# Deformable layer of a fused network: eight taps over 4x4 cells in place of four taps over 4x8, and x hats in two halves

## The chip, the cores and the metric

The kernel runs on one core of one Trainium2 chip. The metric is the device time of one execution in microseconds, the median of several runs. Engine names: PE is TensorE (PEld its weight load), DVE is VectorE, ACT is ScalarE, POOL is GpSimd, SP is SyncE, which here only issues DMAs. Everything is fp32.

## The reference, cut to what matters

The network has four residual layers on x of shape 8 x 384 x 32 x 32 (samples, channels, height, width): a state-space layer, a deformable convolution, a state-space layer with an MLP, and a displacement layer. Only the second is touched. Its core, cut:

```python
def sample(py, px):            # bilinear; corners outside the image count 0
    y0, x0 = floor(py), floor(px)
    dy, dx = py - y0, px - x0
    return (corner(y0, x0, (1 - dy) * (1 - dx)) + corner(y0, x0 + 1, (1 - dy) * dx)
            + corner(y0 + 1, x0, dy * (1 - dx)) + corner(y0 + 1, x0 + 1, dy * dx))
def deform_block(x, ow, ob, dw, pw, pb, K):
    offsets = conv2d(x, ow, ob, K // 2)          # 2*K*K channels: dy, dx of each tap
    acc = 0
    for k in range(K * K):                       # the taps; same offsets for all 128 channels
        acc += sample(gy + ky[k] + offsets[2 * k], gx + kx[k] + offsets[2 * k + 1]) * dw[k]
    return conv2d(acc, pw, pb, 0)                # 1x1
# layer: groupnorm, channels split in three groups of 128 with K = 3, 5, 7, outputs
# concatenated, times a squeeze-and-excite weight, plus x
```

## The kernel before, in words

**The sampling as a matrix product.** A bilinear corner weight is a product of two hats, max(0, 1 - |py - yc|) and max(0, 1 - |px - xc|), for the pixel (yc, xc) read. So for each tap the sampled image of 128 channels is a matrix product: rows of the image's pixels (the contraction, on the partitions) with a matrix "pixel by output position" of hat products. Offsets are bounded (RAD is 2, 3, 4 for K = 3, 5, 7), so a small cell of pixels can only reach a small window of output positions. A cell before is 4 rows by 8 columns, 32 pixels; four taps are stacked on the 128 partitions (a *quad*, `QUADS`). The image has 8 x 4 such cells. K*K = 9, 25, 49 taps give 2, 6, 12 quads, and one tap left over, which is done alone with whole rows as cells (4 rows x 32 pixels, 8 cells).

**The pipeline of one quad.** SP fetches the positions of its four taps from DRAM, each row copied to the 32 partitions of its tap (`positions`, tile `fpyx`, two buffers; the DRAM rows are written by `offsets` or `fir_end` and called `fposd`). ACT makes hats of x (`fhx`, L1573 Abs and L1579 Relu) and of y (`fhy`, L1586 Abs and L1591 Relu); one Abs per cell column or row, one Relu for the tile, two buffers each. DVE multiplies the pixels of the cells, 8 x 128 channels at a time, by the tap's weights (`weigh`, L1609, out `fxk`, four buffers, from the cells `fxt` and the broadcast weights `fwk`) and hat by hat (`product`, L1626, out `fsm`, five buffers, one instruction for cells of equal height). PE multiplies (`products`, L1657), each cell into its window of `wacc`: five PSUM banks of 16 rows that overlap by 8 rows[...].

**A block** is one sample b and one group g (K = 3, 5, 7). At its end ACT copies outer rows of `wacc` out (`sums_act`, L1381), DVE adds the others (`sums`, L1386), both into `fdsb`, and only then may PE start the next block, as `wacc` has one buffer. Then PE does the 1x1 convolution, and ACT and DVE the squeeze.

**Units and slots.** A quad is done in two units, the upper and the lower four rows of cells; a unit is `(b, g, j, h)`. There are 6, 14 and 26 units for K = 3, 5, 7: 46 a sample, 368 in all. The list of units is the clock of the layer. In slot u PE does unit u, DVE weighs and multiplies unit u+1, ACT makes the hats of unit u+2 (x and y hats of a quad together with its upper half), and SP fetches positions four units ahead. The order on PE, DVE and ACT is as written (`tc.manual_schedule`); POOL's and SP's follows from the scheduler. All else is put into slots by `put(slot, place, ...)`: places `act0`, `pe0`, `dve0` stand ahead of the unit's work on that engine, `act1`, `dve1`, `pe1` behind it. With s0 the first slot of a block:

```python
put(s0 - 5, "dve1", cells_map)      # image reordered to cells, fxp<-fxn, 8 copies on POOL (L1335)
put(s0 - 4, "pe1", rows_pe)         # transposes, pixels to partitions
put(s0 - 3, "act0", cells_out)      # to DRAM (fxd)
for q in range(4):                  # and back, copied for the four taps: 4 tiles fxt4 of 0.5 MB
    put(s0 - 1 + q // 2, "dve0", cells_in, q)
put(end, "act0", sums_act)
put(end, "dve0", sums)
```

The offset convolutions are put beside the units of the blocks ahead: K = 7 in slots 0 to 13 of its own sample (`fir`, L1267), K = 5 in slots 34 to 39 and K = 3 at once in slot 5 (`conv`, L1305), both for the next sample. Slots are counted here from the first 3x3 unit of a sample; the 5x5 block starts at slot 6, the 7x7 block at slot 20.

The functions that the change touches, and what calls them:

Of the kernel before, what the change touches and what calls it, by code (L numbers as in the profile page):

```python
# [15 lines left out]
P = 128  # L16
# [36 lines left out]
NX = 4  # L53
# [8 lines left out]
HXN, HYN, SMN = 2080, 1792, 896  # L62
# [3 lines left out]
def box(y, x, h=2, w=2):  # L66
# [3 lines left out]
QUADS = {  # L70
    3: [box(-1, -1), [(-1, 1), (0, 1), (1, 0), (1, 1)], [(1, -1)]],
    5: [box(y, x) for y in (-2, 0) for x in (-2, 0)] + [box(2, -2, 1, 4), box(-2, 2, 4, 1), [(2, 2)]],
    7: [box(-3, -3), box(-3, -1), box(-1, -3, 1, 4), box(-3, 2), box(-1, 2), box(-3, 1, 4, 1)]
    + [box(0, -3), box(2, -3), box(0, -1, 4, 1), box(2, 0), box(2, 2), box(1, 0, 1, 4), [(0, 0)]],
# [14 lines left out]
def taps_of(K):  # L89
    return [(y + K // 2) * K + x + K // 2 for q in QUADS[K] for y, x in q]  # L90

# [5 lines left out]
class Net:  # L97
# [956 lines left out]
    def deform_fast(self, src, dst):  # L1054
        tc, nc, ins = self.tc, self.nc, self.ins
        with ExitStack() as ctx:
# [9 lines left out]
            for g, K in enumerate(KS):  # L1066
                K2, (n, st, cols) = K * K, CONV[K]
                rows = 2 * K2
                queue = nc.scalar if K == 7 else nc.sync
                ow = wp.tile([P, K * NFIR if n == 1 else K2, rows if n == 1 else st], F32, name=f"fow{K}")  # L1070
                ob = wp.tile([P, 1], F32, name=f"fob{K}")
                obk = wp.tile([P, 1], F32, name=f"fobk{K}")
                grid = wp.tile([P, cols], F32, name=f"fgrid{K}")
                for t in (ob, obk, grid) + ((ow,) if n > 1 else ()):
                    nc.gpsimd.memset(t, 0.0)
                if n == 1:
                    self.fir_weights(ow, ins[f"ow{K}"])
                else:
                    queue.dma_start(out=ow[:, :, :rows], in_=ins[f"ow{K}"])
                for i in range(n):  # L1080
                    r = slice(i * st, i * st + rows)
                    queue.dma_start(out=ob[r], in_=ins[f"ob{K}"])
                    queue.dma_start(out=obk[r], in_=ins["c_cols"][:rows, Q_K + g : Q_K + g + 1])
                    queue.dma_start(out=grid[r], in_=ins["c_grid"][:rows, i * cols : (i + 1) * cols])
                if n == 1:
                    nc.gpsimd.tensor_scalar(grid[:rows], grid[:rows], obk[:rows], None, ALU.add)
                nc.vector.tensor_tensor(obk, obk, ob, ALU.add)
                nq = K2 // 4
                wk = wp.tile([P, nq + 1, P], F32, name=f"fwk{K}")
                for t in range(4):  # L1090
                    queue.dma_start(
                        out=wk[H * t : H * (t + 1), :nq, :],
                        in_=ins[f"dw{K}"][t : 4 * nq : 4, :].partition_broadcast(H),
                    )
                queue.dma_start(out=wk[:, nq, :], in_=ins[f"dw{K}"][4 * nq, :].partition_broadcast(P))
                self.f[K] = (ow, ob, obk, grid, wk)
# [8 lines left out]
            self.cell = wp.tile([P, 13], F32, name="cell")  # L1105
# [13 lines left out]
            for b in range(self.nb):  # L1119
                for g in range(G):  # L1120
                    first[b, g] = len(units)
                    units += [(b, g, j, h) for j in self.order(g) for h in range(2)]
# [12 lines left out]
            with tc.manual_schedule(engines=engines):  # L1135
                for u in range(min(slots), max(slots) + 1):
# [4 lines left out]
                    now, after, hats, grid = (unit(u + k) for k in (0, 1, 2, 4))  # L1141
                    if grid and grid[3] == 0:
                        self.positions(*grid)
# [5 lines left out]
                    if dve:  # L1149
                        dve.pop(0)()  # L1150
# [4 lines left out]
                    if hats:  # L1155
                        self.unit_hats(*hats)
# [30 lines left out]
    def block_steps(self, b, g, first, put, weights, src, dst):  # L1187
# [10 lines left out]
        end = first[b, g + 1] if g < G - 1 else first[b, 0] + sum(2 * len(QUADS[k]) for k in KS)  # L1198
# [51 lines left out]
        def fir_sum():  # L1250
            xs = s["xs"] = self.q1.tile([P, H, W // 2], F32, name="fxs")
# [20 lines left out]
        def fir_take(part):  # L1272
            ps = s["ps"][:used]
            if part == 0:
                s["fs"] = self.q1.tile([P, HL], F32, name="ffs")
                nc.scalar.activation(s["fs"][:used], ps, AF.Identity, bias=ob[:used])
                return
# [52 lines left out]
        def cells_map():  # L1330
            xp = s["xp"] = self.q1.tile([P, L], F32, name="fxp")
            x5 = xg().rearrange("p (by yl bx xl) -> p by yl bx xl", yl=4, bx=NX, xl=W // NX)
            p5 = xp.rearrange("p (by yl xl bx) -> p by yl bx xl", yl=4, bx=NX, xl=W // NX)
            for by in range(NT):
                nc.gpsimd.tensor_copy(p5[:, by], x5[:, by])  # L1335
# [17 lines left out]
        def cells_in(q):  # L1353
            xt = s[q] = self.q1.tile([P, NX, 2, P], F32, name="fxt4", tag="fxt4", bufs=4)
            src = s["xd"].rearrange("(c x) y o -> c x y o", x=NX)[:, :, 2 * q : 2 * q + 2]
            n = P // NX
            for t in range(4):
                nc.sync.dma_start(out=xt[n * t : n * (t + 1)], in_=src)
# [91 lines left out]
        if g == 0:  # L1450
            t = s0 - 2 * len(QUADS[KS[-1]])
# [34 lines left out]
        for q in range(4):  # L1486
            put(s0 - 1 + q // 2, "dve0", cells_in, q)
# [29 lines left out]
    def order(self, g):  # L1517
        n = len(QUADS[KS[g]])
        return [n - 1] + list(range(n - 1))

# [8 lines left out]
    def ends(self, g):  # L1529
        last = {}  # L1530
        for j in self.order(g):
            _, _, yw, xw = self.windows(g, j)
            for half in range(2):
                for bx in range(len(xw)):
                    for by in range(4 * half, 4 * half + 4):
# [4 lines left out]
    def windows(self, g, j):  # L1540
        K = KS[g]
        taps, R = QUADS[K][j], RAD[K]
        one = len(taps) == 1
        bw, nbx = (W, 1) if one else (8, NX)
# [6 lines left out]
    def positions(self, b, g, j, half):  # L1551
        s = self.state[b, g]
        taps = QUADS[KS[g]][j]
        pyx = s["pyx", j] = self.q2.tile([P, 2, L], F32, name="fpyx", tag="fpyx")
        n = P // len(taps)
        for t, _ in enumerate(taps):
            self.nc.sync.dma_start(
                out=pyx[n * t : n * (t + 1)],
                in_=s["posd"][8 * j + 2 * t : 8 * j + 2 * t + 2, :].partition_broadcast(n),
            )  # L1560

    def unit_hats(self, b, g, j, half):
        nc, s = self.nc, self.state[b, g]
        taps, one, yw, xw = self.windows(g, j)
        pyx = s["pyx", j]
        if half == 0:
            hx = self.q2.tile([P, HXN], F32, name="fhx", tag="fhx")
            at, hx_at = 0, []
            px = pyx[:, 1, :].rearrange("p (h w) -> p h w", w=W)
            for bx, (xa, xb) in enumerate(xw):  # L1570
                w = xb - xa
                bias = self.cell[:, 12:13] if one else self.cell[:, 8 + bx : 9 + bx]
                nc.scalar.activation(  # L1573
                    hx[:, at : at + H * w].rearrange("p (h w) -> p h w", w=w), px[:, :, xa:xb],
                    AF.Abs, bias=bias,
                )
                hx_at.append(at)
                at += H * w
            nc.scalar.activation(hx[:, :at], hx[:, :at], AF.Relu, bias=self.col(Q_ONE), scale=-1.0)  # L1579
            s["hx", j] = hx, hx_at  # L1580
        hy = self.q2.tile([P, HYN], F32, name="fhy", tag="fhy")
        at, hy_at = 0, {}
        for by in range(4 * half, 4 * half + 4):
# [3 lines left out]
                hy[:, at : at + (yb - ya) * W], pyx[:, 0, ya * W : yb * W], AF.Abs, bias=bias  # L1587
# [4 lines left out]
        s["hy", j, half] = hy, hy_at  # L1592


    def unit_dve(self, b, g, j, half):
# [3 lines left out]
        hx, hx_at = s["hx", j]  # L1599
        hy, hy_at = s["hy", j, half]  # L1600
        xk = s["xk", j, half] = []
        sets = s["sets", j, half] = []

        def weigh():
            for q in (2 * half,) if one else (2 * half, 2 * half + 1):
                t = self.q2.tile([P, 2 * NX, P], F32, name="fxk", tag="fxk", bufs=4)
                n = 4 if one else 2 * NX
                x = s["xt1"][:, 4 * half : 4 * half + 4, :] if one else s[q].rearrange("p x y o -> p (x y) o")
                nc.vector.tensor_tensor(t[:, :n], x, wk[:, j : j + 1, :].to_broadcast([P, n, P]), ALU.mult)  # L1609
                xk.append(t)  # L1610

        def product(bx, part):
# [4 lines left out]
            for by in part:  # L1617
# [17 lines left out]
            sets.append((bx, part, sm, sm_at))  # L1635

        bys = range(4 * half, 4 * half + 4)
        parts = [bys[:2], bys[2:]] if one else [bys]
        return [weigh] + [
            lambda bx=bx, part=part: product(bx, part) for bx in range(len(xw)) for part in parts  # L1640
        ]

    def unit_pe(self, b, g, j, half):
        nc, s = self.nc, self.state[b, g]
        taps, one, yw, xw = self.windows(g, j)
        xk = s["xk", j, half]
        ends = self.ends(g)

        def products(bx, part, sm, sm_at):
            xa, xb = xw[bx]  # L1650
            w = xb - xa
            for by in part:
                ya, yb = yw[by]
                o = self.bank(ya)
                k = xk[0][:, by % 4] if one else xk[(by - 4 * half) // 2][:, 2 * bx + by % 2]
# [8 lines left out]
        return [lambda a=a: products(*a) for a in s["sets", j, half]]  # L1664
# [255 lines left out]
def lay_out(inputs):  # L1920
# [49 lines left out]
    cell = [4 * np.arange(NT)[None, :] + p[:, None] % 32 // 8, 8 * np.arange(NX)[None, :] + p[:, None] % 8]  # L1970
    cell.append(p[:, None] % NX * (W // NX) + p[:, None] % W // NX)
# [26 lines left out]
```

## Time and profile before

| what | value |
|---|---|
| median of 3 runs | 9035.51 us (9035.41 to 9037.79) |
| the profiled execution: time, span | 9039.51 us, 9037.7 us |
| mean granted TensorE clock in it | 0.914 |
| deformable layer in the span | first matmul of L1657 at 2881.6 us, last at about 5469 us |
| columns of all L1657 matmuls, all L1626 products | 852,912 each |
| L1657 PE, busy | 1663.5 us, twice 5312 records |
| L1626 DVE, L1609 DVE, busy | 1170.1 us, 785.7 us |
| L1573 and L1586 ACT (Abs), busy | 407.6 us, 645.1 us |

The profile is of one execution, so a sum over its rows is compared with its own time, 9039.51 us. An fp32 matmul leaves two records in the trace. "Busy" counts the union of an engine's instructions, the mean ns of one its own length, which for pipelined matmuls is more than the distance from one to the next. Idle time before a group is put down to the instruction whose end released it.

### The profile page before, as it was taken

What the parts mean: (1) busy time and instruction counts of PE and PEld (TensorE: products, weight loads), DVE (VectorE), ACT (ScalarE), POOL (GpSimd) and SP (SyncE); (2) the same over time, 40 slices, a digit from 0 to 9 for tenths busy, and PEclk for the clock granted to TensorE, in tenths of its full rate; (3) what the DMA queues carried; (4) which work ended last, traced back from release to release, by engine and by line L of the source; (5) the groups of instructions that cost most, each with busy time, mean ns of one, the idle gap of its engine ahead of it and who ended that gap; (6) DMA issues with size and microseconds to landing.
All of it is one profiled execution on the core that took longest, in us unless ns stands there. A gap on an engine that the chain in (4) does not pass through costs nothing. (4 is left out here: it accounts for less than half of the span.)

```text
span 9037.7 us, 92386 instructions
## 1 busy us (share of the span) xinstructions
PE 7614.4 (84%) x29176; PEld 3845.3 (43%) x29176; DVE 7588.7 (84%) x8309; ACT 6390.0 (71%) x10237; POOL 5766.8 (64%) x3554
## 2 busy tenths in 40 slices
PE   7888888888876999999999995688888888888876
PEld 2232232232323777777777773233333333333333
DVE  6999999999994878887887885898888989888872
ACT  6777777777774777777877885677767777776750
POOL 6999999999993011011101103898998989899954
PEclk8899899899888999999999997899999999999988
DMA  4545545545544454454454443566666666666656
GB/s 129 123 121 123 124 122 123 124 122 123 122 117 105 96 130 106 104 133 107 111 125 118 110 116 97 124 150 148 152 149 160 151 146 150 145 155 147 160 142 115
DMA packets 843980, 1157.36 MB, mean 128 GB/s; under 512 B 281490, under 2 KB 483634, under 8 KB 811736
## 3 DMA queue, kind: packets, MB, share of 16 engines
q1 hardware_dynamic: 781380, 1140.92, 52.1%
q10 hardware_dynamic: 62100, 10.44, 0.7%
q8 instruction: 232, 3.80, 0.2%
q14 instruction: 268, 2.20, 0.1%
HBM read 968.17 MB, written 182.91 MB: 127 GB/s over the span
## 5 line engine op out<-in xcount | busy, mean ns | idle before, releaser
L528 POOL TENSOR_TENSOR db<-dub,bc 128x1024 f32<-128x1024 f32 x1536 | 3605.9, 2356 | 375.7 <-DVE hs L540 171.0
L520 ACT ACTIVATE da<-dtb,vec 128x512 f32<-128x512 f32 x3072 | 2122.3, 691 | 604.1 <-DVE hs L553 406.1
L540 DVE TENSOR_TENSOR_SCAN da<-da,db 128x1024 f32<-128x1024 f32 x960 | 2193.1, 2284 | 131.0 <-ACT da L520 80.4
L1657 PE MATMUL wacc<-fsm,fxk 128*128 128x221 f32 (+34 forms) x10624 | 1663.5, 316 | 155.0 <-DVE fsm L1626 114.3
L1657 PEld LDWEIGHTS wacc<-fsm,fxk 128*128 128x128 f32 x10624 | 1576.3, 196 | 304.5 <-DVE fsm L1626 173.8
L1335 POOL COPY fxp<-fxn 128x128 f32<-128x128 f32 x192 | 218.9, 1274 | 2144.5 <-DVE fxn L1236 1404.8
L540 DVE TENSOR_TENSOR_SCAN hs<-da,db 128x1024 f32<-128x1024 f32 x576 | 1314.8, 2283 | 195.5 <-POOL db L513 80.0
L1626 DVE TENSOR_TENSOR fsm<-fhy,fhx 128x170 f32<-128x170 f32 (+42 forms) x3216 | 1170.1, 428 | 304.4 <-PE wacc L1657 257.1
L551 POOL TENSOR_TENSOR hs<-hs,bc 128x1024 f32<-128x1024 f32 x576 | 1357.0, 2356 | 32.6 <-ACT st L546 32.6
L553 DVE TENSOR_TENSOR hs<-da,bc 128x1024 f32<-128x1024 f32 x960 | 1175.0, 1224 | 128.4 <-PE y L563 78.2
L563 PE MATMUL y<-hs,cols 128*32 128x512 f32 x6144 | 964.9, 643 | 288.9 <-POOL hs L551 264.7
L1586 ACT ACTIVATE fhy<-fpyx,cell 128x416 f32<-128x416 f32 (+9 forms) x1280 | 645.1, 575 | 392.1 <-DVE fsm L1626 392.0
L1609 DVE TENSOR_TENSOR fxk<-fxt,fwk 128x1024 f32<-128x1024 f32 (+1 forms) x688 | 785.7, 1179 | 4.3 <-DMA fxt<-fxd 4.1
L563 PEld LDWEIGHTS y<-hs,cols 128*32 128x32 f32 x6144 | 189.8, 113 | 1002.3 <-issue 494.9
L640 PE MATMUL ps_m<-hid,wm 128*128 128x512 f32 x1152 | 549.2, 631 | 61.7 <-ACT hid L635 27.7
L621 PE MATMUL ps_h<-t,wm 128*128 128x512 f32 x1152 | 530.8, 605 | 47.9 <-DVE sp_e L453 30.7
L1591 ACT ACTIVATE fhy<-fhy,cols 128x1344 f32<-128x1344 f32 (+10 forms) x368 | 530.7, 1442 | 12.0
L353 PE MATMUL ps_in<-xn,winr 128*128 128x512 f32 x576 | 327.5, 715 | 173.9 <-ACT xn L342 125.6
L1573 ACT ACTIVATE fhx<-fpyx,cell 128x544 f32<-128x544 f32 (+10 forms) x664 | 407.6, 685 | 0.0
L640 PEld LDWEIGHTS ps_m<-hid,wm 128*128 128x128 f32 x1152 | 226.2, 202 | 394.1 <-issue 282.6
L1267 PE MATMUL ps_off<-fxn,fow 128*98 128x465 f32 (+10 forms) x896 | 385.4, 579 | 0.0
L621 PEld LDWEIGHTS ps_h<-t,wm 128*128 128x128 f32 x1152 | 215.7, 192 | 366.3 <-issue 271.5
(216 smaller groups left out, 9881.2 us busy)
## 6 DMA issues: line engine op xcount, KB each, us to landing
dtb<-dtd SPq DMA_DIRECT2D x768, 256.0 KB
dub<-dtd SPq DMA_DIRECT2D x768, 256.0 KB
fpyx<-fposd SPq DMA_DIRECT2D x640, 256.0 KB
wm<-in_w SPq DMA_DIRECT2D x96, 768.0 KB
bc<-bcd SPq DMA_DIRECT2D x256, 256.0 KB
x<-x SPq DMA_DIRECT2D x71, 768.0 KB
dtd<-dt SPq DMA_DIRECT2D x192, 256.0 KB
dtd<-sp_e SPq DMA_DIRECT2D x192, 256.0 KB
```

What stands on the lines that cost most here:

```text
L520: nc.scalar.activation(da[:, i, :], s["dtb", j][:, k, :], AF.Exp, scale=na[:, j, n + i : n + i + 1])
L528: nc.gpsimd.tensor_tensor(db, du, s["bc"][p][:, 0], ALU.mult)
L540: nc.vector.tensor_tensor_scan(h1, da1, db1, 0.0, ALU.mult, ALU.add)
L551: nc.gpsimd.tensor_tensor(s["hs", m], s["hs", m], c, ALU.mult)
L553: nc.vector.tensor_tensor(hs_tile(s, m), s["da", m], c, ALU.mult)
L563: nc.tensor.matmul(s["y"][k * IP : (k + 1) * IP, :], sel, s["hs", p * NSUB + k][:, i, :], start=mlp and p == 0 and i == 0, stop=p == NQP - ...
L621: nc.tensor.matmul(ps, s["w1", q][:, k, f * P : (f + 1) * P], s["t"][:, k, :], start=(k == 0), stop=(k == G - 1))
L640: nc.tensor.matmul(ps, s["w2", q][:, f, o * P : (o + 1) * P], s["hid", q][:, f, :], start=(f == 0), stop=(f == 3))
L1586: nc.scalar.activation(hy[:, at : at + (yb - ya) * W], pyx[:, 0, ya * W : yb * W], AF.Abs, bias=bias)
L1609: nc.vector.tensor_tensor(t[:, :n], x, wk[:, j : j + 1, :].to_broadcast([P, n, P]), ALU.mult)
L1626: nc.vector.tensor_tensor(self.sub(sm, at, [(r * w, n), (w, r), (1, w)]), self.sub(hy, hy_at[by] + xa, [(r * W, n), (W, r), (1, w)]), self ...
L1657: nc.tensor.matmul(a[:, ya - 4 * o : yb - 4 * o, xa:xb], k, self.sub(sm, sm_at[by], [(w, yb - ya), (1, w)]), start=o not in s["open"], sto ...
```

## The change

- A cell is 4 x 4 pixels, 16 partitions, and eight taps are stacked (an *octet*, `OCTETS`). The taps are grouped anew: 1, 3, 6 octets and one single tap for K = 3, 5, 7. The image has 8 x 8 cells.
- An octet is done in four units (left or right half of the cell columns, upper or lower half of the rows; `parts`, `blocks`), the single tap in two. There are again 6, 14, 26 units, 46 a sample. A unit still is 16 matmuls for an octet, or 4 for the single tap, with windows narrower by four columns for the same taps.
- Hats of x are made in two halves (`hats_x`), one for each two units; hats of y in two halves (`hats_y`), each kept for two units that do not follow one another: the units of an octet run upper left, lower left, upper right, lower right. A table `hats` says in which slot each is made, for an octet that starts at slot u: x left in u-3, y upper in u-2, y lower in u-1, x right in u. Within one slot x hats come first. They still stand behind the slot's unit and ahead of its `act1` work.
- Positions are fetched five slots ahead of an octet (four ahead of a single tap), eight DMAs of 16 partitions in place of four of 32.
- The weighing is done inside a unit's list, one instruction ahead of every second product, not both ahead of the first; `fxk` has three buffers for four.
- `cells_map` is one DVE copy with a strided write in place of eight POOL copies. The four cell tiles (`fxt8`) are 1 MB each, written by eight DMAs, and their loads are put one slot earlier.
- `fxs` and `ffs` share a buffer, and the weight tiles `fwk` are loaded by eight broadcasts in place of four.

The diff, cut to its core:

```diff
-NX = 4
+NO = 8
+CW = 4
+NX = W // CW
+CELL = 4 * CW
...
-HXN, HYN, SMN = 2080, 1792, 896
+HXN, HYN, SMN = 1856, 1792, 832
...
-                    units += [(b, g, j, h) for j in self.order(g) for h in range(2)]
+                    units += [(b, g, j, h) for j in self.order(g) for h in range(self.parts(g, j))]
+            hats, loads = {}, {}
+            for u, (b, g, j, h) in enumerate(units):
+                if h == 0:
+                    one = self.parts(g, j) == 2
+                    loads[u - (4 if one else 5)] = b, g, j
+                    for t, fn, k in (
+                        ((-2, self.hats_x, 0), (-2, self.hats_y, 0), (-1, self.hats_y, 1))
+                        if one
+                        else ((-3, self.hats_x, 0), (-2, self.hats_y, 0), (-1, self.hats_y, 1), (0, self.hats_x, 1))
+                    ):
+                        hats.setdefault(u + t, []).append((fn, b, g, j, k))
...
-                    now, after, hats, grid = (unit(u + k) for k in (0, 1, 2, 4))
-                    if grid and grid[3] == 0:
-                        self.positions(*grid)
+                    now, after = unit(u), unit(u + 1)
+                    if u in loads:
+                        self.positions(*loads[u])
...
-                    if dve:
-                        dve.pop(0)()
...
-                    if hats:
-                        self.unit_hats(*hats)
+                    for fn, *args in sorted(hats.get(u, ()), key=lambda h: h[0] == self.hats_y):
+                        fn(*args)
...
-            for by in range(NT):
-                nc.gpsimd.tensor_copy(p5[:, by], x5[:, by])
+            x4 = xg().rearrange("p (y bx xl) -> p y bx xl", bx=NX, xl=CW)
+            nc.vector.tensor_copy(xp.rearrange("p (y xl bx) -> p y bx xl", bx=NX, xl=CW), x4)
...
-            xt = s[q] = self.q1.tile([P, NX, 2, P], F32, name="fxt4", tag="fxt4", bufs=4)
...
-            for t in range(4):
-                nc.sync.dma_start(out=xt[n * t : n * (t + 1)], in_=src)
+            xt = s[q] = self.q1.tile([P, 4, 4, P], F32, name="fxt8", tag="fxt8", bufs=4)
...
+            for t in range(NO):
+                nc.sync.dma_start(out=xt[CELL * t : CELL * (t + 1)], in_=src)
...
-            put(s0 - 1 + q // 2, "dve0", cells_in, q)
+            put(s0 - 2 + q // 2, "dve0", cells_in, q)
...
-        bw, nbx = (W, 1) if one else (8, NX)
+        bw, nbx = (W, 1) if one else (CW, NX)
...
-        def weigh():
-            for q in (2 * half,) if one else (2 * half, 2 * half + 1):
-                t = self.q2.tile([P, 2 * NX, P], F32, name="fxk", tag="fxk", bufs=4)
...
+        def weigh(k):
+            t = self.q2.tile([P, 8, P], F32, name="fxk", tag="fxk", bufs=3)
+            n = 4 if one else 8
+            x = s["xt1"][:, 4 * part : 4 * part + 4] if one else s[part][:, 2 * k : 2 * k + 2].rearrange("p x y o -> p (x y) o")
...
+        def both(bx, bys, k):
+            if k is not None:
+                weigh(k)
+            product(bx, bys)
+
+        if one:
+            work = [(0, ys[:2], 0), (0, ys[2:], None)]
+        else:
+            work = [(bx, ys, (bx - xs[0]) // 2 if bx % 2 == 0 else None) for bx in xs]
+        return [lambda a=a: both(*a) for a in work]
```

## The prediction

> **What bounds the kernel now.** I read the busy line and the costliest groups of the page first. All products of the deformable layer are in three groups: matmuls at L1657, the hat products at L1626, the weighing at L1609. Their hats are made at L1573 to L1591.
>
> ```profile
> PE 7614.4 (84%) x29176; PEld 3845.3 (43%) x29176; DVE 7588.7 (84%) x8309; ACT 6390.0 (71%) x10237; POOL 5766.8 (64%) x3554
> L1657 PE MATMUL wacc<-fsm,fxk 128*128 128x221 f32 (+34 forms) x10624 | 1663.5, 316 | 155.0 <-DVE fsm L1626 114.3
> L1335 POOL COPY fxp<-fxn 128x128 f32<-128x128 f32 x192 | 218.9, 1274 | 2144.5 <-DVE fxn L1236 1404.8
> L1626 DVE TENSOR_TENSOR fsm<-fhy,fhx 128x170 f32<-128x170 f32 (+42 forms) x3216 | 1170.1, 428 | 304.4 <-PE wacc L1657 257.1
> L1609 DVE TENSOR_TENSOR fxk<-fxt,fwk 128x1024 f32<-128x1024 f32 (+1 forms) x688 | 785.7, 1179 | 4.3 <-DMA fxt<-fxd 4.1
> ```
>
> The view of the matmuls by tile puts the layer between 2881.6 and 5469 us: 2587 us for eight samples, 46 slots (one unit each) a sample. The page averages over two regimes, so next come busy times by stretch of one sample (the fourth): slots 0-13, 14-32, 33-39 and 40-45. Columns: PE, weight loads, DVE, ACT, POOL, granted clock, DMA share, GB/s.
>
> ```profile
> 3862.40:3972.00 109.60, 109.60 (x525) 70.70 (x524) 72.73 (x146) 79.82 (x121) 4.49 (x8) 1.00 0.50 125
> 3972.00:4090.30 118.30, 100.90 (x610) 94.80 (x608) 112.59 (x227) 102.41 (x142) 4.79 (x8) 0.91 0.53 125
> 4090.30:4151.40 61.10, 61.10 (x396) 46.75 (x396) 47.58 (x103) 49.49 (x66) 0.00 (x0) 1.00 0.31 71
> 4151.40:4189.80 38.40, 35.68 (x212) 31.80 (x212) 36.65 (x73) 27.25 (x41) 19.59 (x8) 1.00 0.51 127
> ```
>
> Where an offset convolution shares the slot (first and third row) PE has no idle time: **PE bound**. In the others DVE is busy 95%: **DVE bound**, with ACT close behind. So each slot must be priced by its own engine. Then the waits of the layer (total, times, longest):
>
> ```profile
> ACT fhy L1586 <- DVE fsm L1626: 411.3, 140, 11.6
> DVE fsm L1626 <- PE wacc L1657: 257.1, 278, 5.1
> DVE fdsb L1386 <- ACT fdsb L1381: 62.7, 23, 5.0
> DVE fsm L1626 <- ACT fhy L1591: 41.4, 38, 2.5
> PE wacc L1657 <- DVE fdsb L1386: 39.6, 8, 5.0
> ```
>
> ACT mostly waits for DVE to free hat buffers; it holds DVE up for 41 us. The last line is the end of the 5x5 block, once a sample. The timeline there:
>
> ```profile
> 3999.81 3.30 DVE L1626 TENSOR_TENSOR fsm<-fhy,fhx 128x234 f32<-128x234 f32 x12
> ...
> 4003.14 2.03 ACT L1586 ACTIVATE fhy<-fpyx,cols 128x384 f32<-128x384 f32 x4 [0.32 <-DVE fsm L1626]
> ...
> 4005.21 1.47 ACT L1591 ACTIVATE fhy<-fhy,cols 128x1408 f32<-128x1408 f32 x1
> 4006.58 1.11 ACT L1381 COPY fdsb<-wacc 128x416 f32<-128x416 f32 x3
> ...
> 4007.72 1.80 DVE L1386 TENSOR_TENSOR fdsb<-fdsb,wacc 128x288 f32<-128x288 f32 x4 [2.34 <-ACT fdsb L1381]
> ...
> 4009.67 3.56 PE L1657 MATMUL wacc<-fsm,fxk 128*128 128x256 f32 x6 [4.95 <-DVE fdsb L1386]
> ```
>
> DVE's last product of the block ends at 4003.1; ACT must first make a y hat (3.5 us) before it copies the sums out, and DVE sits idle 2.34 us.
>
> **What the Trainium skill says.** "VectorE: DVE Perf Modes", on the TRN2 errata: an fp32 tensor_tensor takes (N+151)/0.96 ns. The trace agrees: 1216 ns for 1024. Back to back, starts in the timeline lie only N/0.96 + 69 ns apart (759 for 663 elements, 162 for 90); that is the price I use. "TensorE: Matmul & The Clock Gate", on LDWEIGHTS: 128 columns load in about 107 ns. In the trace the starts of matmul records (two a matmul) lie 112 ns apart below 133 columns and 0.843 ns a column above (187 at 221), so small windows stop paying. "ScalarE: Activation LUTs", on ACT_TABLE_LOAD costs: 280 ns + 0.833 a column with a pointer bias, 93 ns of it overlapped in a row. The trace has 603 ns for 384, and four in 2.03 us (0.833 a column + 156 ns).
>
> **The change, part by part.** Columns are counted in both programs' instruction lists.
>
> 1. *Products.* Units (368), matmuls (5312) and weighings (688) stay. Columns fall from 852,912 to 760,976; DVE issues 3280 products for 3216.
>  PE, at max(112, 0.843 N) for two records a matmul: 190.2 to 177.8 us a sample. Of this, 45.1 to 44.0 in slots 0-13 (3x3 units are at the floor already) and 34.2 to 30.3 in slots 33-39: 4.9 us a sample in PE-bound slots. DVE is nearly level in slots 33 to 35, so I take 4.7, times 8 = **-38 us**.
>  DVE, at N/0.96 + 69 ns: units weighed and multiplied in slots 14-32 go from 100.0 to 94.8 us, those of 40-45 from 30.7 to 29.3: 6.5 x 8 = **-52 us**. The PE gain in these slots and the DVE gain in the others are hidden by the bounding engine and count nothing.
> 2. *Hats.* A y half serves two units: L1586 and L1591 go from 506,112 columns each to 294,912, the x hats from 313,600 to 265,728. At 0.833 x 2 ns that is 432 us less ACT work, plus 800 instructions x 156 ns, 557 us in all. It is nearly all hidden beside DVE or PE. What counts is ACT's 41 us hold on DVE; part is in PE-bound slots, 12 us in the slot after the block end (point 4). I take **-10 us** (0 to -25).
> 3. *cells_map* moves from POOL, where it was hidden, to one strided DVE copy of 1024, 24 times. By rows: 0.80 us (L1236, one source, contiguous) to 1.21 us (L1405); a write stride of eight elements could double the latter. I take 1.0. It falls in slots 41, 1 and 15 of each sample; slot 1 is PE bound, so 16 count: **+16 us** (11 to 39).
> 4. *Block ends, an added wait.* In the slot before a block ends, ACT's list now has the x hats of the next block's first octet ahead of the y hats and the copies of L1381. Their buffer comes free only with the old block's last product, the moment T0 = 4003.1 above. Then everything behind them is late by their cost: for 7x7, 1856 columns, 1856 x 0.833 + 4 x 0.156 us, then Relu 1856 x 0.833 + 156 ns: 3.87 us; for 3x3, 1184 columns: 2.75. Queued behind are hats, copies, DVE's adds (L1386) and PE's first matmul of the new block. At the 5x5 end DVE idles 3.8 us more, and gets back 1.6 because the x hats that it waited for two slots later are there: 2.2 x 8 = 18. At the sample's end the convolution covers only the old bubble: 2.75 x 7 = 19. The 3x3 end has 8 us of convolution over it: 0. Sum **+37 us** (0 if the buffer is free earlier; +60 without the return).
> 5. *Loads.* Cell copies grow from 2 to 4 MB a block, 32 SP issues for 16 at 0.75 us (eight took 6.0): 24 us. Positions keep 664 issues but drop from 184 tiles of 1 MB to 104. Net 32 MB less; at the 205 GB/s seen beside the cell loads, 4 MB take 20 us. The cells are issued one slot earlier, and the quarters are wanted one slot after another (5 to 8 us each) instead of two at once. I take 0. The x load and positions queued behind these issues on SP stay ahead of use by about two slots.
> 6. *Buffers.* fxk goes from 4 to 3, but its second weighing then waits for the same matmuls as the product after it (fsm, five buffers): 0. fxs and ffs share a tile; the reader is done by then: 0.
> 7. *Start, once.* cells_map now stands on DVE behind the 5x5 offsets, which waited for PE until 2866.6: +4 us. ACT's four weight broadcasts (10.1 us of issue) become eight with half the bytes: 0 to -5. Together 0.
>
> Sum: -38 - 52 - 10 + 16 + 37 = **-47 us** against the profiled execution of 9039.5 us (span 9037.7), so 8992; the median of the runs is 4.0 lower, so 8989. About 0.2% (18 us) is what a measurement can tell from no change.
>
> **Rivals.**
> A. *The block ends cost nothing* (the octet's x hats run before T0) and the relief of ACT is full: -38 - 52 - 25 + 11 = -104, so 8930. For it: ACT has 30% of free time. Against: two buffers, the older in use until T0.
> B. *Transfers come late: slower.* A block's 4 MB of cells and its positions share one SP queue; if the first octet's cells or positions land after DVE wants them, DVE stops. The point of decision is 47/24 = 2 us a block; at 4 us a block +96, so 9085. For it: DMA ran at full share (205 GB/s) in bursts of 15 us around block starts. Against: before, these waits were 4.1 us in all, and total traffic falls.
> C. *Windows save nothing.* If short rows in PSUM or SBUF cost DVE or PE what the columns save, -90 becomes about -40, and the rest adds: near 9035. Against: spacing in the trace follows N alone, for row widths of 10 to 17; after it is 7 to 16.
>
> **How the numbers follow.** Main case 0.60, A 0.16, B 0.12, C 0.12. The main case spans -47 with ends -85 and +5, from points 2 to 4: 8950 to 9040. A reaches down to 8930, C up to about 9050; B is left out above. Range 8930 to 9050. Faster by over 0.2%: 0.74 (most of main, A); within: 0.13 (C, upper main); slower: 0.13 (B).
>
> **What would show it.** Right: matmul spacing unchanged, so L1657's successor busy about 1560 us; DVE busy unbroken in slots 14-32 with ACT near 70%; at the 5x5 end DVE idle about 6 us ahead of the adds, and ACT's x hats just before; the fxp copy near 1 us on DVE. Wrong: DVE waits for cell or position loads beyond 10 us; ACT still at 87% in slots 14-32; DVE products slower at equal N.

## The result and the profile after

The changed kernel takes **9240.7 us** (median of 4 runs, 9229.3 to 9241.6) where the kernel before takes 9036.7 in the same runs: ratio 1.0222, 95% interval 1.0205 to 1.0240. It is 204 us slower; the forecast was 47 us faster. The profiled execution has a span of 9227.2 us, 189.5 above that of before; it is the fastest of the four runs, so the trace explains 190 of the 204 us. First the page after, its busy line and the product groups:

```profile
PE 7599.7 (82%) x29176; PEld 3783.0 (41%) x29176; DVE 7508.3 (81%) x8397; ACT 5807.9 (63%) x9437; POOL 5548.2 (60%) x3362
...
L1687 PE MATMUL wacc<-fsm,fxk 128*128 128x195 f32 (+21 forms) x10624 | 1621.2, 310 | 362.2 <-DVE fdsb L1396 154.5
...
L1650 DVE TENSOR_TENSOR fsm<-fhy,fhx 128x143 f32<-128x143 f32 (+40 forms) x3280 | 1085.0, 394 | 326.6 <-PE wacc L1687 257.1
...
L1633 DVE TENSOR_TENSOR fxk<-fxt,fwk 128x1024 f32<-128x1024 f32 (+1 forms) x688 | 813.1, 1182 | 47.2 <-PE wacc L1687 23.2
L1594 ACT ACTIVATE fhx<-fpyx,cell 128x416 f32<-128x416 f32 (+10 forms) x664 | 372.0, 629 | 477.5 <-DVE fsm L1650 280.2
```

Every engine does less work than before: DVE 80 us less, ACT 582, and POOL's copies are gone. What grew is idle time: ahead of the layer's matmuls PE idles 362 us, 155 before, and the largest releaser is now the adds at a block's end. The wait list of the layer (engine and line, what it waited for, total us, times, longest):

```profile
ACT fhy L1610 <- DVE fsm L1650: 458.9, 124, 10.3
ACT fhx L1594 <- DVE fsm L1650: 280.2, 67, 9.3
...
DVE fdsb L1396 <- ACT fdsb L1391: 262.0, 24, 26.4
...
ACT fhx L1594 <- DMA fpyx<-fposd: 187.4, 15, 23.0
ACT fdsb L1391 <- DMA x<-fxr: 170.7, 7, 26.5
PE wacc L1687 <- DVE fdsb L1396: 154.5, 14, 21.7
...
PE wacc L1687 <- ACT fhy L1610: 78.2, 8, 10.3
...
DVE fxk L1633 <- DMA fxt<-fxd: 15.1, 7, 3.8
```

Two lines name a transfer and are long: ACT waits 187 us for positions and 171 us, once in each sample but the first, for the **store** of an output tile (x<-fxr). DVE hardly waits for cells. The kernel before had the store's wait too, but short, and the prediction does not mention it:

```profile
ACT fdsb L1381 <- DMA x<-fxr: 31.9, 7, 5.2
```

To place this, the trace's matmuls were cut into the 46 slots of a sample: a slot lasts from the first matmul of its unit to the first of the next. Means over the eight samples (over seven for slot 45), in us (the experiments' columns are used further down):

| slots | before | after | e1 | e2 | e5 | e6 | e7 | e10c |
|---|---|---|---|---|---|---|---|---|
| 0-4 | 34.2 | 34.9 | 34.9 | 34.9 | 34.7 | 34.3 | 34.2 | 34.2 |
| 5 (3x3 ends) | 12.6 | **29.9** | 12.6 | 25.2 | 13.5 | 12.6 | 12.6 | 12.6 |
| 6-13 | 62.4 | 63.1 | 61.3 | 63.4 | 61.4 | 61.3 | 61.3 | 61.3 |
| 14-18 | 28.2 | 26.9 | 26.9 | 26.9 | 26.9 | 26.9 | 26.9 | 26.0 |
| 19 (5x5 ends) | 9.4 | **14.4** | 14.3 | 14.3 | 14.3 | 14.3 | 10.1 | 10.1 |
| 20-24 | 28.9 | 26.6 | 27.0 | 26.4 | 26.3 | 26.5 | 28.2 | 28.2 |
| 25 | 6.4 | **12.2** | 11.8 | 9.4 | 6.8 | 6.8 | 7.0 | 6.8 |
| 26-32 | 44.7 | 43.4 | 42.9 | 43.2 | 41.7 | 41.5 | 42.0 | 42.6 |
| 33-39 | 58.6 | 55.3 | 55.3 | 55.3 | 55.3 | 55.3 | 55.3 | 55.7 |
| 40-44 | 28.9 | 27.6 | 27.6 | 27.6 | 27.6 | 27.6 | 27.6 | 26.8 |
| 45 (7x7 ends) | 9.6 | **13.0** | 13.0 | 13.0 | 13.0 | 13.0 | 10.4 | 10.4 |
| sum | 324.0 | 347.4 | 327.7 | 339.7 | 321.4 | 320.2 | 315.7 | 314.7 |

The loss sits in four slots, all at or just behind a block's end: 5, 19, 25, 45. Elsewhere nearly every stretch is shorter. Slot 5 alone is 17.3 x 8 = 138 us. The same four stretches as in the prediction (sample 4; columns as there) show that no engine bounds the first two any more:

```profile
3921.00:4051.90 130.90, 112.66 (x524) 72.34 (x525) 70.73 (x155) 57.31 (x86) 0.00 (x0) 0.91 0.65 109
4051.90:4176.20 124.30, 99.24 (x610) 91.58 (x608) 108.01 (x227) 74.41 (x106) 0.00 (x0) 0.88 0.63 105
4176.20:4233.90 57.70, 57.44 (x396) 43.09 (x396) 44.80 (x104) 32.11 (x41) 0.00 (x0) 1.00 0.19 39
4233.90:4274.50 40.60, 35.02 (x212) 30.03 (x211) 35.77 (x73) 22.82 (x37) 0.00 (x0) 1.00 0.64 96
```

In the third PE is still busy throughout, in the first it idles 18 of 131 us, all in slot 5. The timeline there (start, us, engine):

```profile
3950.02 26.72 SPq L1368 DMA_DIRECT2D fxt<-fxd  x31
...
3977.47 0.34 SPq L1458 DMA_DIRECT2D x<-fxr  x1
3978.50 7.36 SPq L1580 DMA_DIRECT2D fpyx<-fposd  x8
3985.64 1.14 ACT L1391 COPY fdsb<-wacc 128x352 f32<-128x352 f32 x3 [23.03 <-DMA x<-fxr]
...
3986.81 1.39 DVE L1396 TENSOR_TENSOR fdsb<-fdsb,wacc 128x320 f32<-128x320 f32 x4 [22.88 <-ACT fdsb L1391]
...
3988.35 4.29 PE L1687 MATMUL wacc<-fsm,fxk 128*128 128x224 f32 x8 [18.24 <-DVE fdsb L1396]
```

SP needs 26.7 us to issue the 5x5 block's cell loads. Behind them in its queue stands the store of an output tile, whose value was ready on DVE at 3963.9. That tile, `fxr`, shares its one buffer with `fdsb` (tag "fdsb"), so ACT's copies of the 3x3 sums wait for the store to land, DVE's adds wait for ACT, and PE for DVE: it stands still for 18 us.

With the loads put one slot earlier, all of them now stand ahead of the store. In the kernel before, at the same place, it went out between the two halves of the block's loads:

```profile
3881.26 5.70 SPq L1358 DMA_DIRECT2D fxt<-fxd  x8
3900.12 0.34 SPq L1448 DMA_DIRECT2D x<-fxr  x1
...
3902.71 5.99 SPq L1358 DMA_DIRECT2D fxt<-fxd  x8
```

Slot 25 (from 4120.3 to 4131.9 in this sample) has the same cause with another victim. Positions of a 7x7 octet stand behind the block's 32 loads; ACT waits for them, then DVE 5.2 us for ACT's hats and PE 4.4 us for DVE:

```profile
4084.04 24.98 SPq L1368 DMA_DIRECT2D fxt<-fxd  x32
...
4109.70 30.34 SPq L1580 DMA_DIRECT2D fpyx<-fposd  x22
...
4124.10 2.35 ACT L1594 ACTIVATE fhx<-fpyx,cell 128x352 f32<-128x352 f32 x4 [16.60 <-DMA fpyx<-fposd]
```

Why the issues take so long is seen in the transfers of slot 5's time (busy share of the DMA engines and GB/s in 40 slices):

```profile
DMA  0559999999999999999999999999999999999989
GB/s 19 148 164 169 123 125 134 127 132 125 130 118 127 132 130 130 130 125 123 125 130 134 130 132 118 123 130 125 139 127 132 120 125 125 127 132 127 160 315 435
```

The engines count as full, at 130 GB/s. The first ten issues come mostly 0.47 us apart, the later ones 1.03 us. 128 KB in 1.03 us is 127 GB/s, so SP then issues no faster than the transfers drain. The load of a block takes 30 to 33 us. The kernel before moves half the bytes in two bursts of 5 to 7 us, most of them at 180 to 200 GB/s (packet records). The Trainium skill has this: "SBUF — State Buffer", "Door 1: The DMA port swizzle", says that a transfer's rate depends on how many of the memory's 16 ports its partitions reach, and measures 104 GB/s for partitions 0..15, 189 for 0..31 and 328 for all 128, each for a transfer of 1 MB. This trace agrees in order, not in size: 130 for 128 KB at a time over 16 partitions. The change had gone from DMAs over 32 partitions to DMAs over 16.

### The profile page after: what moved, and what is told of

Its sections match the earlier page's. It is cut to its first block, busy times and chain, and to the rows that moved or that the text cites. A ratio compares the mean times of both kernels' runs of the same rounds, so it can differ in the third digit from the quotient of the medians.

```text
span 9227.2 us, 91792 instructions
## 1 busy us (share of the span) xinstructions
PE 7599.7 (82%) x29176; PEld 3783.0 (41%) x29176; DVE 7508.3 (81%) x8397; ACT 5807.9 (63%) x9437; POOL 5548.2 (60%) x3362
## 5 line engine op out<-in xcount | busy, mean ns | idle before, releaser
L1687 PE MATMUL wacc<-fsm,fxk 128*128 128x195 f32 (+21 forms) x10624 | 1621.2, 310 | 362.2 <-DVE fdsb L1396 154.5
L464 POOL TENSOR_TENSOR dt<-dt,sp_e 128x512 f32<-128x512 f32 x96 | 122.4, 1275 | 2931.7 <-DVE sp_e L456 2931.7
L1687 PEld LDWEIGHTS wacc<-fsm,fxk 128*128 128x128 f32 x10624 | 1504.0, 198 | 543.2 <-DVE fsm L1650 210.9
L1650 DVE TENSOR_TENSOR fsm<-fhy,fhx 128x143 f32<-128x143 f32 (+40 forms) x3280 | 1085.0, 394 | 326.6 <-PE wacc L1687 257.1
L1633 DVE TENSOR_TENSOR fxk<-fxt,fwk 128x1024 f32<-128x1024 f32 (+1 forms) x688 | 813.1, 1182 | 47.2 <-PE wacc L1687 23.2
L1594 ACT ACTIVATE fhx<-fpyx,cell 128x416 f32<-128x416 f32 (+10 forms) x664 | 372.0, 629 | 477.5 <-DVE fsm L1650 280.2
L1610 ACT ACTIVATE fhy<-fpyx,cell 128x416 f32<-128x416 f32 (+9 forms) x640 | 334.9, 595 | 415.4 <-DVE fsm L1650 415.4
L575 PE MATMUL ps_z<-xn,winr 128*128 128x512 f32 x576 | 302.8, 674 | 48.1 <-DVE sp_e L456 48.1
```

The lines of the kernel that those rows point to most:

```text
L1650: nc.vector.tensor_tensor(self.sub(sm, at, [(r * w, n), (w, r), (1, w)]), self.sub(hy, hy_at[by] + xa, [(r * W, n), (W, r), (1, w)]), self ...
L1687: nc.tensor.matmul(a[:, ya - 4 * o : yb - 4 * o, xa:xb], k, self.sub(sm, sm_at[by], [(w, yb - ya), (1, w)]), start=o not in s["open"], sto ...
```

## The experiments

All are timed against the kernel before, in the same runs (9038 to 9040 us); the changed kernel is at 9241. The theory: a block's loads got slow, by twice the bytes and by DMAs of few partitions, and they hurt through what stands behind them in SP's queue, a store and positions. Rivals: the bytes alone; the late cells; the order on ACT at block ends.

**e1: fxr out of fdsb's buffer.**

```diff
-            xp = s["xp"] = self.q1.tile([P, L], F32, name="fxp")
+            xp = s["xp"] = self.q1.tile([P, L], F32, name="fxp", tag="fxp")
...
-            xr = sample["xr"] = self.q1.tile([P, L], F32, name="fxr", tag="fdsb")
+            xr = sample["xr"] = self.q1.tile([P, L], F32, name="fxr", tag="fxp")
```

> The changed kernel, but the tile fxr of the residual (loaded, scaled, stored) takes the buffer of fxp instead of that of fdsb, so that ACT's copies into fdsb no longer wait for the store x<-fxr. Theory (the store stands in SP's queue behind 32 cell loads, and ACT's copies wait for it): slot 5, the end of the 3x3 block, falls from 29.9 us a sample to 12.6 to 14, 7 samples x 17 = -120 us, near 9120; slot 25 stays at 12.2. Rival (the cells themselves come too late, whatever ACT does): the wait moves to DVE's weighing, which waits for fxt<-fxd, and less than 40 us is gained: 9200.

Measured: **9077.8 us**, ratio 1.0045 (1.0028 to 1.0062). Slot 5 is 12.63 us, to the hundredth that of before; slots 6 to 13 also lose what the late start had cost (63.1 to 61.3). The whole of slot 5 was that one wait; the cells did not come too late behind it (DVE waits 16.0 us for them, 15.1 before the edit). Slot 25 stays at 11.8. The gain of 163 us is more than the 120 forecast: the 17 us of slot 5 is a mean over eight samples and was multiplied by seven, and slots 6 to 13 were not counted.

**e2: cells over 128 partitions, first form.** Taps stay in blocks of 16 partitions; the source has a step of 0 over the eight taps, outermost.

```diff
-            for t in range(NO):
-                nc.sync.dma_start(out=xt[CELL * t : CELL * (t + 1)], in_=src)
+            for x in range(4):
+                src = bass.AP(tensor=xd.tensor, offset=xd.offset + ((4 * bx + x) * NT + 4 * by) * P,
+                              ap=[[0, NO], [NX * NT * P, CELL], [1, 4 * P]])
+                nc.sync.dma_start(out=xt[:, x].rearrange("p y o -> p (y o)"), in_=src)
```

> The changed kernel, but each 1 MB cell tile is loaded by four DMAs over all 128 partitions (one per cell column, the taps by a source step of 0) in place of eight over 16 partitions: the same 4 MB a block, the same 2 KB runs, 16 issues for 32. Theory[...]: the loads of a block take under 20 us instead of 33 (over 200 GB/s instead of 127); the wait at slot 5 falls by 14 us or more and the 5.8 us of slot 25 go: about -14 x 7 - 6 x 8 = -146, near 9095. Rival (4 MB is too much for the DMA engines in these slots, however it is cut): 33 us again, and within 10 us of 9240.

Measured: **9166.1 us**, ratio 1.0139 (1.0122 to 1.0156), half of the theory's gain. A 2 KB packet now takes 86 ns (median of the packet records) where it took 253, yet the rate is only 145 GB/s. While the loads shown here ran, the packets' times add up to 8.2 engines at work (all 16 in the changed kernel); the transfers' view shows their share at half:

```profile
DMA  0243555555555555555555579858545848357794
GB/s 18 32 157 127 177 148 141 150 148 146 146 146 146 146 146 146 146 146 146 146 148 148 146 248 339 214 61 207 39 121 150 196 91 162 73 162 253 232 159 87
```

The Trainium skill, "DMA: Bandwidth & Descriptors", "Why a DMA increments its semaphore by 16 and not by 1", gives the reason: a DMA runs on the largest number of engines up to 16 that divides the slowest step's count on both sides. Here that is 8, the count of the source's step over the taps. The trace agrees.

**e3: the kernel before, its loads cut to 16 partitions.**

```diff
             for t in range(4):
-                nc.sync.dma_start(out=xt[n * t : n * (t + 1)], in_=src)
+                for i in range(2):
+                    nc.sync.dma_start(out=xt[n * t + 16 * i : n * t + 16 * i + 16], in_=src[16 * i : 16 * i + 16])
```

> The kernel before, each of its 16 cell loads of a block (32 partitions) cut into two of 16 partitions: the same 2 MB in 1 KB runs, 32 issues for 16. Theory (16 partitions are slow): the 2 MB run at about 127 GB/s instead of 205, 16 us instead of 10, and the wait of ACT for the store at slot 5 (31.9 us in 7 samples) grows by 2 to 6 us a sample: 9050 to 9085. Rival (the partitions don't matter, only the bytes): the rate stays at 205 GB/s and the time within 10 us of 9036.

Measured: **9108.7 us**, ratio 1.0080 (1.0063 to 1.0096), more than forecast. The rate falls to 103 to 125 GB/s with the same bytes, but the place was wrong: the store wait stays at 32.4 us, since the store still goes out between the halves of the loads (3918.6, the second half from 3921.2), and DVE waits for cells instead (68.0 us in 25 waits, mostly in slots 2, 3, 22 and 23). This run doesn't tell few partitions from many small DMAs: its packets are quick (68 ns for 1 KB), and its issues come 0.64 us apart, so the pace of SP alone gives 64 KB in 0.64 us, 102 GB/s. It does show that the kernel before had little room in its loads.

**e4: the first x half of a block behind the copies of the sums.**

```diff
+                    t0 = -2 if u == first[b, g] + 2 else -3
...
-                        else ((-3, self.hats_x, 0), (-2, self.hats_y, 0), (-1, self.hats_y, 1), (0, self.hats_x, 1))
+                        else ((t0, self.hats_x, 0), (-2, self.hats_y, 0), (-1, self.hats_y, 1), (0, self.hats_x, 1))
```

> The changed kernel, but the first x half of the first octet of each block is made one slot later, so that on ACT it stands behind the copies of the old block's sums and not ahead of them. Theory of the prediction with what the slots showed: at the sample's end, where PE bounds the slots that follow, slot 45 falls by about 3.4 us (7 times); at the end of the 5x5 block slot 19 falls by about 4 us but slots 20 to 22 get it back, since ACT's hats after the old block's last product bound the start of the first octet in either order: together -20 to -30 us, near 9212. Rival a (the whole 3.9 and 2.75 us come back): -55 us, 9185. Rival b (the copies wait for something else): no change.

Measured: **9352.4 us**, ratio 1.0346 (1.0329 to 1.0364): all three expectations missed, 112 us slower than the changed kernel. Slots 19 and 45 did fall as the theory said, to 10.1 and 10.4. But slots 0 to 4 grew to 42.0, slot 5 to 36.3, slots 20 to 24 to 34.8. SP's order is left to the scheduler, and it changed. In this run:

```profile
3960.50 0.33 SPq L1581 DMA_DIRECT2D fpyx<-fposd  x1
3960.93 26.61 SPq L1369 DMA_DIRECT2D fxt<-fxd  x32
3988.22 6.18 SPq L1581 DMA_DIRECT2D fpyx<-fposd  x8
```

One position DMA stands ahead of the 32 loads of the 3x3 block and goes out only at 3960.5, when the first matmul of that block comes at 3965.3. In the changed kernel these loads began 15.2 us ahead of the block, here 4.4. The queue's own waits name what held that DMA back: 13.1 us for ACT's y hats (L1611), which read a position tile and end at 3960.47. So it waited for a buffer of positions; that was not tried by itself. DVE then waits 175.7 us for cells, 15.1 in the changed kernel. Whether the deferral is good by itself had to be asked again with a queue that isn't full: e7.

**e5: all ports, all engines.** The partitions of an octet are ordered pixel-tap (partition 8 c + t in place of 16 t + c), so that the outermost step has 16 entries. Against e2:

```diff
-                    ap=[[0, NO], [NX * NT * P, CELL], [1, 4 * P]]
+                    ap=[[NX * NT * P, CELL], [0, NO], [1, 4 * P]]
...
-        for t, _ in enumerate(taps):
...
+        self.nc.sync.dma_start(
+            out=pyx.rearrange("p y l -> p (y l)"), in_=bass.AP(
+                tensor=posd.tensor, offset=posd.offset + 2 * NO * j * L, ap=[[0, n], [2 * L, len(taps)], [1, 2 * L]]))
...
-    at = p[:, None] % CELL
+    at = p[:, None] // NO
```

(and the weights' broadcasts in the same order)

> The changed kernel with the partitions of an octet in the order pixel-tap, not tap-pixel, so that a cell column of all eight taps is one DMA over 128 partitions whose slowest step has 16 entries on both sides (e2 had 8 on the source's): 16 loads of 256 KB a block, and one position DMA of 1 MB an octet in place of eight of 128 KB. fxr still shares the buffer of fdsb. Theory (16 partitions at a time are slow, and e2 was held back by running on half of the DMA engines): packets of 2 KB take about 90 ns as in e2 but on all 16 engines, so the 4 MB of a block take about 16 us instead of 33; the store behind them comes 15 us earlier, slot 5 falls from 29.9 to about 15, slot 25 from 12.2 to about 6.5: -15 x 7 - 6 x 8 = -153, near 9085. Rival (the DRAM side or the number of bytes limits at 145 GB/s, as e2 seems to say): within 15 us of e2's 9166.

Measured: **9019.1 us**, ratio 0.9977 (0.9968 to 0.9986): 222 us below the changed kernel, well past the forecast, which counted slots 5 and 25 alone: slots 6-13 and 26-32 fell by 1.7 us each as well. The 4 MB of a block take 16 to 18 us at 230 to 265 GB/s; slot 5 is 13.5, slot 25 6.8. Packets of 2 KB take 108 ns, so 250 GB/s is 13 engines at work. The number of bytes was not the limit. The changed kernel kept all 16 engines busy, but with packets of 253 ns, so the difference lies in how the transfers are cut. That is the partitions of one DMA, but also its size (256 KB for 128) and the order in which the source is read; these were not tried apart. e5 changes cells and positions together; their shares were not tried apart either.

**e6: e5 and e1 together.**

> As the one before, and fxr in the buffer of fxp as in e1. Theory: the store's wait is gone as in e1 (9078), and beside that the late positions at slot 25 (5.4 us, 8 times) and the slots after it: 9078 - 43 - 10, near 9025, which is below the kernel before (9037). Rival (positions at slot 25 are late for their place in the queue, behind the cells, not for the rate): slot 25 stays above 10 us and the time near 9070.

Measured: **9013.3 us**, ratio 0.9971 (0.9961 to 0.9981); its profile has no wait for positions, the store or cells above 9 us in the layer. With fast loads the shared buffer is nearly harmless: e5 still waits 39 us for the store (31.9 before), and slot 5's convolution covers most of it.

**e7: e6 with the deferral of e4.**

> As e6, and the first x half of a block's first octet one slot later, behind the copies of the sums (the edit of e4, now with loads that no longer fill the queue). Theory: slot 45 falls by 2.6 us (7 times) and slot 19 by 4.3 as in e4, of which slots 20 to 24 take about 4 back: -20 to -30 against e6. Rival (in e4 all of the loss, 8 us in slots 20 to 24 and 7 in slots 1 to 3, came from the deferral itself): slower than e6 by 50 us or more.

Measured: **8977.7 us**, ratio 0.9934 (0.9918 to 0.9951), 36 less than e6. Slot 45 gives 2.6 x 7 = 18, slot 19 gives 4.2 x 8 = 34, slots 20 to 32 take (1.7 + 0.2 + 0.6) x 8 = 19 back. So in e4 the loss came from the queue, not from the order on ACT.

**e8: e6 with cells_map on POOL.**

```diff
-            nc.vector.tensor_copy(xp.rearrange("p (y xl bx) -> p y bx xl", bx=NX, xl=CW), x4)
+            for by in range(NT):
+                nc.gpsimd.tensor_copy(p5[:, by], x5[:, by])
```

> As e6, with cells_map as eight copies on POOL again, as in the kernel before, in place of one DVE copy of 1.1 us. The prediction's point 3: DVE is the bound in slots 15 and 41, not in slot 1, so -1.1 x 16 = -18 us against e6. Rival (DVE's lead over PE in these slots takes it up): no change; or slower, where the transposes wait for POOL.

Measured: **9001.2 us**, ratio 0.9957 (0.9941 to 0.9974), 12 less than e6, two thirds of what was expected: slots 14 to 18 and 40 to 44 are 0.9 and 0.8 shorter, slots 25 to 32 one longer. The two profiled executions differ by 4.8 us only; that of e6 was the fastest of its nine runs, so the 12 us rest on the medians.

**e9c: the changed kernel, its loads spread over four slots.**

```diff
-            put(s0 - 2 + q // 2, "dve0", cells_in, q)
+            put(s0 - 2 + q, "dve0", cells_in, q)
```

> The changed kernel with one edit: its four cell tiles are loaded in four slots (s0-2 to s0+1) and not in two, same DMAs, same bytes. Theory (a slow load hurts by what stands behind it in SP's queue): the store of slot 5 has 8 to 16 loads ahead of it and not 32, slot 5 falls from 29.9 to 13 to 20, and the positions of slot 25 go ahead of the last tile: 9080 to 9130. Rival (the time that all transfers need counts, whatever their order): above 9180.

Measured: **9120.5 us**, ratio 1.0089 (1.0072 to 1.0106), 120 of the 204 back with one index. Slot 5 is 16.0, as forecast. Slot 25 falls to 8.5, but slots 20 to 24 grow to 33.5: at 130 GB/s something has to be late there, now one slot earlier. Here order decided who waited, and the rate that somebody had to.

**e10c: e7 and e8 together.**

> e7 (all ports, own fxr, first x half deferred) with cells_map on POOL as in e8: the two gains add, 8978 - 12 = 8966. Rival (the time that cells_map took on DVE is covered once the blocks start earlier): 8978.

Measured: **8960.6 us**, ratio 0.9915 (0.9898 to 0.9931), 17 below e7: the gains add. With e11c it is the fastest version, 0.85% ahead of the kernel before.

**e11c: e10c with one more ACT task behind the copies at the sample's end.** The single tap's second `hats_y` is called right after the `act0` tasks of the new sample's first slot, no longer one slot earlier (its entry in the table `hats` goes):

```diff
-                    run(u, "act0", "pe0", "dve0")
+                    run(u, "act0")
+                    for k, *args in early:
+                        if k == u:
+                            self.hats_y(*args, 1)
+                    run(u, "pe0", "dve0")
```

> As the best so far (e7 with cells_map on POOL), and at the end of a sample the second y hats of the single 3x3 tap (3.3 us on ACT) stand behind the copies of the old block's sums too. Theory: PE, which bounds the slots that follow, gets wacc 3 us earlier: slot 45 falls from 10.4 to about 7.5, 7 samples: -20, 8946. Rival (DVE's second product of the single tap then waits for these hats, and PE for it): no change, with DVE waiting for fhy in slot 0.

Measured: **8960.6 us**, no change, but for neither reason given. e10c, at the end of a sample:

```profile
4146.31 4.19 PE L1281 MATMUL ps_off<-fxs,fow 128*98 128x512 f32 x10 [1.29 <-DVE fxs L1267]
...
4146.57 1.05 ACT L1399 COPY fdsb<-wacc 128x512 f32<-128x512 f32 x2
...
4150.34 3.03 PE L1696 MATMUL wacc<-fsm,fxk 128*128 128x160 f32 x14
```

and e11c:

```profile
4144.86 1.07 ACT L1406 COPY fdsb<-wacc 128x512 f32<-128x512 f32 x2 [3.99 <-PE wacc L1703]
...
4146.12 4.19 PE L1288 MATMUL ps_off<-fxs,fow 128*98 128x512 f32 x10 [1.29 <-DVE fxs L1274]
...
4150.14 3.02 PE L1703 MATMUL wacc<-fsm,fxk 128*128 128x160 f32 x14
```

The copies do come earlier, by 1.5 us if counted from the old block's last matmul, but between the blocks PE does a piece of the 7x7 offset convolution that waits for DVE's `fxs` and lasts to 4150.3 in both. At this end the convolution is now the bound.

**e12c: the kernel before with the transfers of e6.** Quads in pixel-tap order, one DMA over 128 partitions for each cell column and for a quad's positions, fxr in fxp's buffer:

```diff
-            for t in range(4):
-                nc.sync.dma_start(out=xt[n * t : n * (t + 1)], in_=src)
+            for x in range(NX):
+                src = bass.AP(tensor=xd.tensor, offset=xd.offset + (x * NT + 2 * q) * P,
+                              ap=[[NX * NT * P, P // NX], [0, 4], [1, 2 * P]])
+                nc.sync.dma_start(out=xt[:, x].rearrange("p y o -> p (y o)"), in_=src)
```

> The kernel before with the transfers of e6: its quads in the order pixel-tap, each cell column and each quad's positions in one DMA over 128 partitions, fxr in the buffer of fxp. Theory (before, transfers were hidden, with 4 us of DVE's waits and a store wait that the convolution of slot 5 covers): 9020 to 9040. Rival (transfers cost the kernel before as much as they cost the changed one, so that what e6 gains is not the change's): 9000 or below.

Measured: **9041.0 us**, ratio 1.0002 (0.9994 to 1.0011). Before, transfers were hidden and stay so; what e6 gains over the kernel before is the change's own, once its loads are hidden.

## Why the prediction was wrong

**The step that failed is point 5, loads, taken at 0.** Against e6, where no wait for positions, the store or cells adds up to more than 9 us, the changed kernel loses (347.4 - 320.2) x 8 = 217 us to them, 9 us a block. Three things went wrong in it:

- *The rate.* 4 MB were priced at the 205 GB/s of the kernel before, 20 us. The DMAs had half as many partitions each; measured 130 GB/s, 32 us. The table of the Trainium skill would have given 104. The 205 itself may be no limit of the transfers: SP issued those loads 0.64 us apart, and 128 KB in 0.64 us is 205 GB/s. That was not tried.
- *The queue.* "The x load and positions queued behind these issues stay ahead of use by about two slots" did not hold for the positions (no wait for an x load shows in the layer). Behind undrained loads the issuing itself slows (1.03 us an issue, not 0.75), and positions that went out at 4109.7 let ACT start its hats only at 4124.1, after 16.6 us of waiting: slot 25.
- *What else stands in it.* The output store was not in the list of things behind the loads. The kernel before already showed its wait, 31.9 us in 7 samples, covered by slot 5's convolution; the prediction does not mention it. With the loads one slot earlier all 32 went out ahead of the store, where 8 of 16 had, and the convolution no longer covered the wait.

Also the sign to look for, "DVE waits for cell or position loads beyond 10 us", looked at the wrong engine: DVE waited 15 us for cells, ACT 358 for positions and the store. **Rival B** had the direction and a part of the mechanism, positions late behind the cells, at 4 us a block and a chance of 0.12. The larger part, slot 5 with 138 us, is a store that holds up ACT, and that stands in no rival.

**The other points**, by slots of e6 against before (times 8):

- *Products and hats.* PE-bound slots 6-13 and 33-39: -1.1 - 3.4 = -4.5 before rounding, **-36 us**, forecast -38. DVE-bound slots 14-18, 20-32 and 40-44: 137.1 to 129.4, **-62 us**; forecast -52, with -10 for hats, +16 for cells_map and -13 for what block ends return, -59. Rival C (short windows save nothing) is out. As forecast, the starts of matmul records lie 111 to 112 ns apart below 133 columns and 0.85 ns a column above; yet PE's busy time in the layer is 1621 us, 1580 in e6, and not 1560.
- *cells_map.* The copy takes 1.11 us (forecast 1.0); off DVE it gave 12 us (16).
- *Block ends.* The mechanism was right, the size low: slot 19 +4.9 x 8 and slot 45 +3.4 x 7, **+63 us**, forecast 50 ahead of the return. At the 5x5 end, where PE had idled 4.95 us before:

```profile
4083.08 2.44 ACT L1594 ACTIVATE fhx<-fpyx,cell 128x352 f32<-128x352 f32 x4 [2.15 <-DMA fxd<-fxt]
...
4087.30 1.95 ACT L1610 ACTIVATE fhy<-fpyx,cols 128x384 f32<-128x384 f32 x4
...
4090.60 1.11 ACT L1391 COPY fdsb<-wacc 128x448 f32<-128x448 f32 x3
...
4091.75 1.93 DVE L1396 TENSOR_TENSOR fdsb<-fdsb,wacc 128x320 f32<-128x320 f32 x4 [7.07 <-ACT fdsb L1391]
...
4093.82 7.23 PE L1687 MATMUL wacc<-fsm,fxk 128*128 128x288 f32 x16 [10.31 <-ACT fhy L1610]
```

x hats, y hats, copies, in that order, and DVE idle for 7.1 us (forecast about 6). The trace puts the end of PE's wait down to ACT's next y hats, which end within 0.01 us of DVE's adds. e7 took most of it back: 4.2 of slot 19's 4.9 us and 2.6 of slot 45's 3.4. Rival A is out as well.

- *Buffers.* `fxk` with three buffers shows 23.2 us of waits for PE, while the products' wait for PE stays at 257.1 as before; a cost was not seen in any slot, nor was it tried by itself.

Without point 5 the sum was sound, term by term: forecast -47, e6 measured -34 in its profile (9004.0 against 9037.7) and -26 between medians; the difference to -47 is mostly the block ends.

## What to carry to other kernels

When an edit cuts transfers into DMAs over fewer partitions, price their rate anew, by partitions and by the steps of both access patterns; here the rate of the old ones did not carry over. Then list everything behind them in the same queue, stores included, above all when an edit moves them earlier, and follow each to the buffer that it frees: a store that shares a buffer with an accumulator's copy can stop PE. A wait that is covered today is a margin with a size; write that size down beside it.

## What the runs showed that was not expected

- The same 4 MB in the same 2 KB runs moved at 130, 145 and 250 GB/s: over 16 partitions; over 128 with a source step of 8 outermost; over 128 with 16 outermost. Packets took 253, 86 and 108 ns (medians).
- A one-slot move on ACT (e4) cost 112 us, because SP's queue came in another order; with room in that queue the same move gained 36.
